# A recurrent cell on one Trainium2 core: biases as one row through TensorE, wx's first part in two column halves, and another deal of the inner weight sums

## The chip, the core and the metric

The kernel runs on one core of one Trainium2 chip. A core has five engines that run side by side and wait for one another through semaphores: TensorE (PE in the profile, with its weight loads as PEld) for matmuls, VectorE (DVE), ScalarE (ACT), GpSimd (POOL) and SyncE (SP), which here only issues transfers. Sixteen DMA engines move data between the device's memory and the on-chip memory. The metric is the device time of one execution in microseconds; the time before is the median of three runs.

## The reference

A recurrent cell goes over 512 steps for a batch of 8, with 512 inputs and 512 units, and its states are added to the input:

```python
def step(h, x_t):
    fused = sigmoid(concatenate([x_t, h], axis=-1) @ w_W + w_b)
    hidden_state, output_state = split(fused, 2, axis=-1)
    memory_state = x_t @ wx_W + wx_b + hidden_state * (h @ wh_W + wh_b)
    h_new = output_state * h + (1.0 - output_state) * tanh(memory_state)
    return h_new, h_new
...
out = x + scan(step, h0=cond_1024, over the 512 steps)
```

Everything is in 32-bit floats. There are three bias vectors: `w_b` (two gates), `wx_b` and `wh_b`.

## The kernel before

**Layout.** The 512 units are spread over 128 partitions as 4 groups (index `j`) of 32 partitions, so a matmul with a weight tile of 32 columns fills one quarter of the partitions, and four of them, one for each `j`, run beside one another. The contraction over 512 is cut into 4 chunks (index `k`). `wx` holds the weights that meet the input (384 columns for each `k` and `j`), `wa` and `wd` those that meet the state (256 and 128 columns). The banks of PSUM are named `xp0`, `xp1`, and `A`, `D`, `H` of two sets, `banks[0]` and `whole[1]`.

**The steps.** For every time step `i` TensorE multiplies the state by `wa` and `wd` (banks A, D and H, in the order of the string `ORDER`), and behind that does a few units of the input's part for later steps (x work): three units in most steps, four in the steps of `PLAIN` and in one of sixteen later. VectorE transposes what comes out (the transposes `tr`, `tz`, `md1`), ScalarE applies the sigmoids and the tanh, and two scans on VectorE give the new state `hT`, which TensorE's next step waits for. GpSimd adds the input to the state (`ot`), and SP stores it.

**The input's part.** For steps 0 to 31 it is made by plain passes: `x_pass(g, k)` multiplies four steps (group `g`) of the input by chunk `k` of `wx`. A bank is first filled with the bias by ScalarE (`seed`), and the passes add to it. From step 15 on the x work is done by a scheme with fewer products, for which sums of pieces of `wx` are wanted: `tw` (`weight_sum`, before step 0) and `ti` (`inner_weight`). VectorE makes the last 46 half pieces of `ti` at the ends of steps 0 to 15; the list `late` says which in which step.

**The start.** All engines begin together. SP issues the transfers in the order of the code, each up to 0.5 us of its time: `head` (the biases, already repeated over all partitions, then the first half chunk of the input and the first state), chunk 0 of `wx`, a piece of the input, chunks 1 to 3 of `wx`, `wa`, and `wd`; from the ninth on, the issue of one waits until the one eight places ahead has landed. TensorE meanwhile clears the banks: matmuls with the bfloat16 tile `none`, which is all zeros, and for bank D of `whole[1]` two matmuls with the float tile `zeros`. ScalarE waits for `head` and then seeds five banks from it. TensorE's first passes go through the chunks `k` in order, with the groups 0 to 3 inside (two groups in the last chunk), and then begins step 0, whose matmuls are dealt between passes that are still owed (the string `FIRST`); its D part needs `wd`. VectorE fills tiles, copies the first state out of `head` and makes the `tw` sums as the chunks of `wx` land. GpSimd copies parts of the bias from `head` into `xs` and `off`.

From the making of the banks on, the order on each engine is that of the code, and a wait holds back all that stands behind it on its engine.

Of the kernel before, what the change touches and what calls it, by code (L numbers as in the profile page):

```python
# [7 lines left out]
F32 = mybir.dt.float32  # L8
# [5 lines left out]
P = 128  # L14
NQ = 4
GS = 4
B = 8
# [15 lines left out]
HALF = 192  # L33
# [32 lines left out]

DONE = (5, 9, 14)

COLS = slice(64, 448)

SC = slice(128, 512)
# [5 lines left out]
def tile_cond_rnn_residual(  # L77
    ctx: ExitStack,
    tc: tile.TileContext,
    x: bass.AP,  # L80
    xh: bass.AP,
    wx_d: bass.AP,
    wa_d: bass.AP,
    wd_d: bass.AP,
# [31 lines left out]
    nc = tc.nc  # L116
# [4 lines left out]
    const = ctx.enter_context(tc.tile_pool(name="const", bufs=1))  # L121
# [6 lines left out]


    NX = NQ * TC * B // 2  # L130
    head = const.tile([P, 512 + NX + NQ * B], F32, name="head")
    nc.sync.dma_start(out=head, in_=xh)
    bias = head[:, :512]
    hin = head[:, 512 + NX :].rearrange("p (k b) -> p k b", k=NQ)

    def load_x(c, half=slice(0, 2), ks=slice(0, NQ)):

        if c < NCH:
            if c not in xins:
                xins[c] = xin_p.tile([P, 2, NQ, TC * B // 2], F32, tag="xin", name=f"xin_{c}")  # L140
            nc.sync.dma_start(
                out=xins[c][:, half, ks],
                in_=x[c].rearrange("p (e k n) -> p e k n", e=2, k=NQ)[:, half, ks],
            )

    def x_of(c, k, t, n):

        e, t = divmod(t, TC // 2)
        if c == 0 and e == 0:
            first = head[:, 512 : 512 + NX].rearrange("p (k n) -> p k n", k=NQ)  # L150
            return first[:, k, t * B : (t + n) * B]
        return xins[c][:, e, k, t * B : (t + n) * B]


    wx = const.tile([P, NQ, NQ, 384], F32, name="wx")
    for k in range(NQ):
        nc.sync.dma_start(out=wx[:, k], in_=wx_d[k])
        if k == 0:
            load_x(0, 1)

    wa = const.tile([P, NQ, NQ, 256], F32, name="wa")
    for k in range(NQ):
# [3 lines left out]
    wd = const.tile([P, NQ, NQ, 128], F32, name="wd")  # L166
# [16 lines left out]
    hd0 = [[pair(n, f"hd0{n}{i}", m, 3) for i in range(2)] for n, m in (("A", B), ("B", 32))]  # L183
    zeros = const.tile([P, 512], F32, name="zeros")
    nc.vector.memset(zeros, 0.0)  # L185
    none = const.tile([P, 128], BF16, name="none")
    nc.vector.memset(none, 0.0)

# [7 lines left out]
    idle = const.tile([P, IDLE], F32, name="idle")  # L196

    tw = const.tile([P, 4, 2, NQ, HALF], F32, name="tw")
    ti = const.tile([P, 7, 4, 2, HALF], F32, name="ti")
# [14 lines left out]
    whole = [{n: psum.tile([P, 512], F32, name=f"{n}{q}") for n in BANKS} for q in range(2)]  # L214
    banks = [{n: whole[q][n][:, :w] for n, w in BANKS.items()} for q in range(2)]
    xps = [psum.tile([P, 512], F32, name=f"xp{q}") for q in range(2)]

    def mm(out_, lhsT, rhs, start=False):
        nc.tensor.matmul(  # L219
            out_, lhsT, rhs, start=start, stop=False, skip_group_check=True  # L220
        )


    for t_ in xps + [whole[1]["H"], whole[1]["A"]] + list(banks[0].values()):
        mm(t_, none, none[:, :1].broadcast_to([P, t_.shape[1]]), start=True)
    for n in range(2):
        mm(whole[1]["D"], zeros[:, :128], zeros, start=n == 0)

    def bank_of(g):

# [60 lines left out]
    def seed(g):  # L291

        at = COLS if g else slice(0, 512)
        nc.scalar.copy(bank_of(g)[:, at], bias[:, at])

    def passes(*todo):

        for v in todo:
            x_pass(*v)
            yield  # L300
# [151 lines left out]
    def take(it, n=None):  # L452
        while n is None or n > 0:
            if next(it, it) is it:
                return
            n = None if n is None else n - 1
# [35 lines left out]
    jobs, late = {}, {}  # L492
# [2 lines left out]
        jobs.setdefault(i, []).extend(todo)  # L495

    halves = [(n, p, h) for n in (0, 2, 1, 3) for p in range(7) for h in range(2) if n or p > 4]
    for at in range(0, len(halves), 3):
        for n, p, h in halves[at : at + 3]:
            todo = late.setdefault(at // 3, [])  # L500
            if h and todo and todo[-1][:2] == (n, p):
                todo[-1] = (n, p, slice(0, 2))
            else:
                todo.append((n, p, slice(h, h + 1)))
    drains = {}
    for c in range(2, NCH):
        w0 = TC * c - LEAD
# [16 lines left out]
    for i in range(T):  # L524
        g, s = divmod(i, GS)
        c, t = divmod(i, TC)
        ps = banks[g % 2]
        if c > 0 and t in (1, 4, 7, 10):
            e, k = divmod(t // 3, 2)
# [5 lines left out]
        for n in (ORDER if i else FIRST).split():  # L535
# [6 lines left out]
            bank, k = n[0], int(n[1])  # L542
# [272 lines left out]
```

## Time and profile before

| | |
|---|---|
| median of the runs | 1627.92 us (1627.80 to 1628.28) |
| the profiled execution | 1627.71 us, of which its span is 1625.9 |
| mean granted TensorE clock | 1.000 |
| busy: TensorE, VectorE, ScalarE, GpSimd | 99%, 87%, 63%, 33% |
| first x pass on TensorE, from the start of the span | 6.30 us |
| first matmul of step 0 on TensorE | 16.23 us |
| one step later on | 3.12 us |

How to read it: rows of the timeline give the start, the length, the engine, the line of the kernel, the operation with its output and input, shapes and a count, and in brackets how long the engine had been idle before it and what ended that. A row of stretches gives the stretch, its length, TensorE's busy time with the count of its matmuls, the granted clock, the busy share of the DMA engines and GB/s. A row of a tile gives the count, the shortest, the median and the longest time in ns, and the first and the last start in us. One matmul of the code in 32-bit floats is two in the profile. In the DMA view a queue's row gives packets, MB, and the time that the packets took as a share of 16 engines over the stretch; the line of sizes counts packets cumulatively. A busy TensorE is not TensorE at its peak, since matmuls overlap and their ends are modelled.

### The profile page before, as it was taken

The page shows a single profiled execution, that of the slowest core. Times are in us where ns is not written, and L with a number is a line of the kernel's source. Part 1 is how long each engine was busy: PE and PEld are TensorE (multiplying, and loading weights), DVE is VectorE, ACT ScalarE, POOL GpSimd, SP SyncE. Part 2 cuts the span into 40 slices and gives each one's busy share as a digit, 9 for nine tenths or more (in the row PEclk, how much of TensorE's full clock was granted, in tenths as well). Part 3 has the DMA queues.
Part 4 walks back from the last instruction along what each step waited for, and adds up shares of the span by engine and source line. Part 5 has one row for each costly group of instructions (what it writes and reads, how often), then busy time and mean ns, then how long its engine had stood idle before and what let it go on. Part 6 is the DMA issues. An engine that isn't in the chain of part 4 may idle for free.

```text
span 1625.9 us, 120027 instructions
## 1 busy us (share of the span) xinstructions
PE 1616.3 (99%) x49211; PEld 1308.3 (80%) x49211; DVE 1411.1 (87%) x11757; ACT 1023.8 (63%) x6033; POOL 539.1 (33%) x1443
## 2 busy tenths in 40 slices
PE   9999999999999999999999999999999999999998
PEld 5888888888888888888888888888888888888876
DVE  8988888888888888888888888888888888888887
ACT  4666666666666666666666666666666666666665
POOL 2323333333333333333333333333333333333321
PEclk9999999999999999999999999999999999999999
DMA  4011111111111111111111111111111111110110
GB/s 192 12 40 33 29 37 38 43 32 33 31 43 39 35 34 31 39 38 39 33 29 37 38 43 32 30 35 43 38 33 34 32 39 38 39 34 25 31 35 10
DMA packets 66217, 62.04 MB, mean 38 GB/s; under 512 B 9856, under 2 KB 64000, under 8 KB 65664
## 3 DMA queue, kind: packets, MB, share of 16 engines
q1 hardware_dynamic: 65664, 54.35, 12.7%
q8 instruction: 385, 6.31, 1.7%
q14 instruction: 168, 1.38, 0.3%
HBM read 14.96 MB, written 8.39 MB: 14 GB/s over the span
## 4 chain that ended last, share of the span: by engine, by line
PE 98%; DVE 1%; issue 0%; ACT 0%; DVEq 0%
PE A L219 49%; PE D L219 27%; PE xp L219 16%; PE H L219 7%; DVE tr L577 0%; DVE m L565 0%; DVE md1B L636 0%; DVE hT L565 0%; DVE md1A L592 0%; DVE tz L577 0%; DVE zeros L185 0%; DVE hd0B L629 0%; DVE md1B L592 0%; DVE idle L600 0%; ACT hT L285 0%
## 5 line engine op out<-in xcount | busy, mean ns | idle before, releaser
L219 PE MATMUL A<-wa,hT 128*32 128x256 f32 x16352 | 877.8, 355 | 4.2 <-DVE hT L565 4.2
L219 PEld LDWEIGHTS A<-wa,hT 128*32 128x32 f32 x16352 | 497.5, 123 | 260.2 <-DVE hT L565 135.6
L219 PE MATMUL D<-wd,hT 128*32 128x128 f32 x16384 | 541.0, 273 | 0.0
L219 PEld LDWEIGHTS D<-wd,hT 128*32 128x32 f32 x16384 | 480.4, 122 | 21.8 <-DMA wd<-in_wd_dram 0.5
L731 POOL TENSOR_TENSOR ot<-xin,hT 128x32 f32<-128x32 f32 x503 | 134.4, 267 | 1046.5 <-DVE hT L565 1028.8
L285 ACT ACTIVATE md0A<-tr 128x16 f32<-128x16 f32 x512 | 112.9, 221 | 385.2 <-DVE tr L577 385.2
L285 ACT ACTIVATE hT<-m 128x8 f32<-128x8 f32 x2048 | 324.2, 207 | 46.8 <-DVE m L565 0.4
L577 DVE STREAM_TRANSPOSE tr<-A 128x64 f32<-128x64 f32 x511 | 127.8, 250 | 199.4 <-PE A L219 198.2
L285 ACT ACTIVATE hT<-hT 128x16 f32<-128x16 f32 x1024 | 232.3, 227 | 91.4 <-DVE hT L565 89.9
L219 PE MATMUL H<-wa,hT 128*32 128x64 f32 x8208 | 208.3, 219 | 0.0
L285 ACT ACTIVATE md0B<-tr 128x8 f32<-128x8 f32 x1024 | 160.0, 206 | 42.6 <-DVE tr L577 1.2
L219 PEld LDWEIGHTS H<-wa,hT 128*32 128x32 f32 x8208 | 185.6, 122 | 0.0
L565 DVE TENSOR_TENSOR_SCAN hT<-hd0B,hT 128x24 f32<-128x24 f32 x1024 | 171.4, 208 | 0.8 <-DVE hT L565 0.8
L565 DVE TENSOR_TENSOR_SCAN hT<-hd0A,hT 128x24 f32<-128x24 f32 x1024 | 171.9, 168 | 0.0
L565 DVE TENSOR_TENSOR_SCAN m<-md0B,md1B 128x24 f32<-128x24 f32 x1024 | 154.5, 193 | 0.5 <-issue 0.4
L629 DVE STREAM_TRANSPOSE hd0B<-sz 128x32 f32<-128x32 f32 x1024 | 148.5, 190 | 0.0
L565 DVE TENSOR_TENSOR_SCAN m<-md0A,md1A 128x16 f32<-128x16 f32 x1024 | 142.5, 181 | 5.1
L219 PE MATMUL xp<-ti,si 128*32 128x192 f32 (+1 forms) x3120 | 146.7, 295 | 0.0
L450 POOL TENSOR_TENSOR xs<-ff 128x192 f32<-128x192 f32 x240 | 139.5, 597 | 0.1
L636 DVE STREAM_TRANSPOSE md1B<-A 128x64 f32<-128x64 f32 x511 | 130.1, 255 | 0.0
L285 ACT ACTIVATE hd0A<-tz 128x16 f32<-128x16 f32 x512 | 116.6, 228 | 21.2
L592 DVE STREAM_TRANSPOSE md1B<-H 128x64 f32<-128x64 f32 x512 | 128.3, 251 | 0.0
(110 smaller groups left out, 1861.0 us busy)
## 6 DMA issues: line engine op xcount, KB each, us to landing
ff<-tt SPq DMA_DIRECT2D x120, 96.0 KB, 2.6
ff<-tt SPq DMA_DIRECT2D x120, 72.0 KB, 2.2
out_dram<-ot SPq DMA_DIRECT2D x128, 64.0 KB, 1.8
xin<-in_x_dram SPq DMA_DIRECT2D x112, 64.0 KB, 2.1
ff<-ff SPq DMA_DIRECT2D x60, 96.0 KB, 2.1
ff<-ff SPq DMA_DIRECT2D x60, 72.0 KB, 2.7
wx<-in_wx_dram SPq DMA_DIRECT2D x4, 768.0 KB, 7.3
wa<-in_wa_dram SPq DMA_DIRECT2D x4, 512.0 KB, 11.1
```

Source lines behind the costliest of these rows:

```text
L219: nc.tensor.matmul(out_, lhsT, rhs, start=start, stop=False, skip_group_check=True)
L285: inst = nc.scalar.activation(out_, in_, func, **kw).ins
L450: nc.gpsimd.tensor_tensor(to, a, b, ALU.add)
L565: return nc.vector.tensor_tensor_scan(*[t_[:, :, c_].rearrange("p n c s -> p (n c s)") for t_ in (out_, d0, d1)], 0.0, ALU.mult, ALU.add,).ins
L577: inst = nc.vector.transpose(t_.rearrange("p c n -> p (c n)"), raw[n][hf]).ins
L592: inst = nc.vector.transpose(md1[hf][g % 2][:, :, :, hf].rearrange("p n c -> p c n"), raw["h"][hf]).ins
L629: nc.vector.transpose(hd0[1][i % 2][:, :, q, 2], sz[:, 32 * q : 32 * q + 32]).ins
L636: nc.vector.transpose(md1[1][g % 2][:, :, :, 0].rearrange("p n c -> p c n"), ps["A"][:, :HU])
L731: pool_done[i + 1] = nc.gpsimd.tensor_tensor(ot[:, t], x_of(c, slice(0, NQ), t, 1), hTs[(i + 1) % NH][:, :, :, B * s1 : B * s1 + B, 2].rea ...
```

## The change

It has three parts, all at the start.

First, `head` no longer carries the biases. They come as one row of 2048 floats on one partition, by a transfer of their own that stands first on SP's queue. The row is put into the memory of `ti`, which is not otherwise written before the inner sums. Four matmuls with a column of ones (`ones`, one partition by 32) repeat it over the partitions of the first bank `xp0`, and ScalarE copies that bank into a new tile `bias`, from which everything reads that read `head` before. Bank `xp0` then already holds its bias, so its seed goes; the other seeds stay. Bank D of `whole[1]` is cleared by a `none` matmul like the other banks, and the two `zeros` matmuls go.

Second, chunk 0 of `wx` is loaded in two halves of 192 columns of each `j`, the piece of the input between them, and its passes are done in the same halves: all four groups with the first half, then all four with the second.

Third, the list `SUMS` says how many half pieces of `ti` each of the first sixteen steps makes; before it was three in each and one in the last. The pieces keep their order.

```diff
+SUMS = (3, 3, 3, 2, 2, 4, 2, 4, 4, 4, 3, 2, 3, 2, 4, 1)
...
-    head = const.tile([P, 512 + NX + NQ * B], F32, name="head")
+    ti = const.tile([P, 7, 4, 2, HALF], F32, name="ti")
+    rows_b = ti[:1].rearrange("p a n j c -> p (a n j c)")[:, : NQ * 512]
+    nc.sync.dma_start(out=rows_b, in_=bias_d)
+    head = const.tile([P, NX + NQ * B], F32, name="head")
     nc.sync.dma_start(out=head, in_=xh)
-    bias = head[:, :512]
-    hin = head[:, 512 + NX :].rearrange("p (k b) -> p k b", k=NQ)
+    bias = const.tile([P, 512], F32, name="bias")
+    hin = head[:, NX:].rearrange("p (k b) -> p k b", k=NQ)
...
     wx = const.tile([P, NQ, NQ, 384], F32, name="wx")
-    for k in range(NQ):
-        nc.sync.dma_start(out=wx[:, k], in_=wx_d[k])
-        if k == 0:
+    for v in range(2):
+        nc.sync.dma_start(out=wx[:, 0, :, HALF * v : HALF * v + HALF], in_=wx0_d[v])
+        if v == 0:
             load_x(0, 1)
+    for k in range(1, NQ):
+        nc.sync.dma_start(out=wx[:, k], in_=wx_d[k - 1])
...
+    ones = const.tile([1, 32], F32, name="ones")
+    nc.vector.memset(ones, 1.0)
...
-    for t_ in xps + [whole[1]["H"], whole[1]["A"]] + list(banks[0].values()):
+    for t_ in xps + list(whole[1].values()) + list(banks[0].values()):
         mm(t_, none, none[:, :1].broadcast_to([P, t_.shape[1]]), start=True)
-    for n in range(2):
-        mm(whole[1]["D"], zeros[:, :128], zeros, start=n == 0)
+    for j in range(NQ):
+        mm(xps[0][32 * j : 32 * j + 32], ones, rows_b[:, 512 * j : 512 * j + 512])
+    nc.scalar.copy(bias, xps[0])
...
-    for g in range(5):
+    for g in range(1, 5):
         seed(g)
-    take(passes(*[(g, k) for k in range(NQ) for g in range(2 if k == NQ - 1 else 4)], (4, 0)))
+    take(passes(*[(g, 0, slice(v, v + HALF)) for v in (0, HALF) for g in range(4)]))
+    take(passes(*[(g, k) for k in range(1, NQ) for g in range(2 if k == NQ - 1 else 4)], (4, 0)))
...
-    for at in range(0, len(halves), 3):
-        for n, p, h in halves[at : at + 3]:
-            todo = late.setdefault(at // 3, [])
+    for at, n_ in enumerate(SUMS):
+        todo = late.setdefault(at, [])
+        for n, p, h in halves[:n_]:
...
+        del halves[:n_]
...
-    xh_d = c_(_np.concatenate([_np.repeat(bias_d, 32, 0), xd[0, :, : 2 * TC * Bn], h0], 1))
+    xh_d = c_(_np.concatenate([xd[0, :, : 2 * TC * Bn], h0], 1))
+    bias_d = c_(bias_d.reshape(1, -1))
+    wx0_d = c_(_np.stack([wx_d[0, :, :, :192], wx_d[0, :, :, 192:]]))
+    wx_d = c_(wx_d[1:])
```

What this makes of the order on the engines, at the places that matter below. SP's queue at the start, before (`xin_74` and `xin_81` are the input's first two chunks):

```order
L132 DMA head<-in_xh_dram 128x800
L157 DMA wx<-in_wx_dram 128x1536
L141 DMA xin_74<-in_x_dram 128x256
L157 DMA wx<-in_wx_dram 128x1536 x3
L163 DMA wa<-in_wa_dram 128x1024
L141 DMA xin_81<-in_x_dram 128x256
L163 DMA wa<-in_wa_dram 128x1024 x3
L167 DMA wd<-in_wd_dram 128x1536
```

and SP's queue now:

```order
L137 DMA ti<-in_bias_dram 1x2048
L139 DMA head<-in_xh_dram 128x288
L164 DMA wx<-in_wx_dram 128x4x192
L148 DMA xin_77<-in_x_dram 128x256
L164 DMA wx<-in_wx_dram 128x4x192
L168 DMA wx<-in_wx_dram 128x1536 x3
L172 DMA wa<-in_wa_dram 128x1024
L148 DMA xin_85<-in_x_dram 128x256
L172 DMA wa<-in_wa_dram 128x1024 x3
L176 DMA wd<-in_wd_dram 128x1536
```

The bias row stands first, `head` is shorter, and chunk 0 of `wx` is two transfers of 4 runs of 192 floats on each partition; what follows keeps its order.

TensorE behind the first matmuls with `none`, before (`xp_175` and `xp_176` are the banks xp0 and xp1, `H_174` and `A_172` the banks of groups 2 and 3):

```order
L219 MATMUL H_171<-none 128x64
L219 MATMUL D_173<-zeros 128x512 x2
L219 MATMUL xp_175<-wx,head 32x384 x4
L219 MATMUL xp_176<-wx,head 32x384 x4
L219 MATMUL H_174<-wx,xin_74 32x384 x4
L219 MATMUL A_172<-wx,xin_74 32x384 x4
L219 MATMUL xp_175<-wx,head 32x384 x4
```

and TensorE at the same place now (`xp_180`, `xp_181`, `H_179` and `A_177` are the same four banks):

```order
L229 MATMUL H_176<-none 128x64
L229 MATMUL xp_180<-ti,ones 32x512 x4
L229 MATMUL xp_180<-wx,head 32x192 x4
L229 MATMUL xp_181<-wx,head 32x192 x4
L229 MATMUL H_179<-wx,xin_77 32x192 x4
L229 MATMUL A_177<-wx,xin_77 32x192 x4
L229 MATMUL xp_180<-wx,head 32x192 x4
L229 MATMUL xp_181<-wx,head 32x192 x4
L229 MATMUL H_179<-wx,xin_77 32x192 x4
L229 MATMUL A_177<-wx,xin_77 32x192 x4
L229 MATMUL xp_180<-wx,head 32x384 x4
```

The `zeros` matmuls are gone, the four with `ones` stand in their place, and chunk 0 has twice the passes at half the columns.

On ScalarE the first copy at the start now reads bank xp0, which TensorE writes, where it read `head`, and the four seeds behind it read its output.

VectorE at the end of step 4, before (the first row is the last scan of the state, `ti` the inner sums, `tr_5` the first transpose of step 5):

```order
L565 TENSOR_SCALAR hT_95<-hd0B_108,hT_94 128x24 x2
L338 TENSOR_TENSOR ti<-tw 128x384
L338 TENSOR_TENSOR ti<-tw 128x192
L710 MEMSET idle 128x1 x2
L577 STREAM_TRANSPOSE tr_5_850<-A_172 128x64
```

and at the same place now:

```order
L579 TENSOR_SCALAR hT_99<-hd0B_112,hT_98 128x24 x2
L349 TENSOR_TENSOR ti<-tw 128x192 x2
L724 MEMSET idle 128x1 x2
L591 STREAM_TRANSPOSE tr_5_874<-A_177 128x64
L606 STREAM_TRANSPOSE md1A_107<-A_177 128x64
```

Step 4 ends with two half pieces where it had three (a whole piece of 384 columns counts two).

More of the change, by code (lines that the diff above doesn't have):

```diff
@@ L80, in tile_cond_rnn_residual @@
     x: bass.AP,
+    bias_d: bass.AP,
     xh: bass.AP,
+    wx0_d: bass.AP,
     wx_d: bass.AP,
@@ L149, in x_of @@
         if c == 0 and e == 0:
-            first = head[:, 512 : 512 + NX].rearrange("p (k n) -> p k n", k=NQ)
+            first = head[:, :NX].rearrange("p (k n) -> p k n", k=NQ)
             return first[:, k, t * B : (t + n) * B]
@@ L198, in tile_cond_rnn_residual @@
     tw = const.tile([P, 4, 2, NQ, HALF], F32, name="tw")
-    ti = const.tile([P, 7, 4, 2, HALF], F32, name="ti")
     so = [const.tile([P, 4, 2, 2, 32], F32, name=f"so{q}") for q in range(2)]
@@ L504, in tile_cond_rnn_residual @@
                 todo.append((n, p, slice(h, h + 1)))
+        del halves[:n_]
+    assert not halves
     drains = {}
@@ L801 @@
     for name, a in (
-        ("x", xd), ("xh", xh_d), ("wx", wx_d), ("wa", wa_d), ("wd", wd_d), ("wd3", wd3_d),
+        ("x", xd), ("bias", bias_d), ("xh", xh_d), ("wx0", wx0_d), ("wx", wx_d), ("wa", wa_d), ("wd", wd_d), ("wd3", wd3_d),
     ):
```

## The prediction

> **What bounds the kernel now.** I read the page's busy shares and its chain first, then the chain in order of time for the first 50 us, then the steps, then the start in the timeline, and last the DMA view, since the change touches nothing but the start and the sums in the first sixteen steps.
>
> ```profile
> PE 1616.3 (99%) x49211; PEld 1308.3 (80%) x49211; DVE 1411.1 (87%) x11757; ACT 1023.8 (63%) x6033; POOL 539.1 (33%) x1443
> ...
> PE 98%; DVE 1%; issue 0%; ACT 0%; DVEq 0%
> ```
>
> TensorE carries 98% of the chain. To see whether single steps hide something, I cut the trace at the starts of successive `tr<-A` transposes (one per step) and asked for TensorE's busy time between them.
>
> ```profile
> 27.71:30.87 3.16, 3.16 (x116) 1.00 0.03 8
> 30.87:33.97 3.10, 3.10 (x113) 1.00 0.02 5
> 33.97:37.16 3.19, 3.19 (x116) 1.00 0.08 21
> 37.16:40.43 3.27, 3.27 (x124) 1.00 0.03 8
> 40.43:43.91 3.48, 3.48 (x131) 1.00 0.02 5
> 43.91:47.02 3.11, 3.11 (x116) 1.00 0.02 5
> ...
> 78.67:81.79 3.12, 3.12 (x108) 1.00 0.02 5
> ```
>
> A step with three units of x work takes 3.10 to 3.12 us and one with four units (steps 5 to 9 and 14) 3.27: a period set by TensorE's own work. Only the first rows deviate: step 2 by 0.05, step 4 by 0.08, and steps 6 and 7 together by 0.05 (3.48 + 3.11 against 2 x 3.27). About 500 steps are left alone by the change, so all that can move is the start, here in the timeline (start us, length us, engine, line).
>
> ```profile
> 0.74 0.39 SPq L132 DMA_DIRECT2D head<-in_xh_dram  x1
> ...
> 1.93 0.15 PEld L219 LDWEIGHTS <-none 128*128 128x128 bf16 x1 [0.28 <-issue]
> ...
> 2.36 0.15 PEld L219 LDWEIGHTS <-none 128*128 128x128 bf16 x1 [0.28 <-issue]
> ...
> 3.60 2.77 PE L219 MATMUL D<-zeros 128*128 128x512 f32 x4
> ...
> 4.93 0.48 ACT L294 COPY H<-head 128x384 f32<-128x384 f32 x1
> ...
> 5.35 0.47 ACT L294 COPY A<-head 128x384 f32<-128x384 f32 x1
> ...
> 6.30 0.16 PEld L219 LDWEIGHTS xp<-wx,head 128*32 128x32 f32 x8 [0.76 <-ACT A L294]
> ...
> 8.72 0.33 SPq L167 DMA_DIRECT2D wd<-in_wd_dram  x1
> ...
> 8.91 1.47 PE L219 MATMUL xp<-wx,head 128*32 128x384 f32 x16
> ...
> 17.59 0.19 PEld L219 LDWEIGHTS xp<-wa,hT 128*32 128x32 f32 x8 [0.51 <-DMA wa<-in_wa_dram]
> ...
> 20.68 0.84 PEld L219 LDWEIGHTS D<-wd,hT 128*32 128x32 f32 x32 [0.53 <-DMA wd<-in_wd_dram]
> ```
>
> The x passes begin at 6.30, as the `zeros` matmuls leave TensorE (3.60 + 2.77 = 6.37), chunk k=1 of wx is used from 8.91, and step 0 stands still for `wd` at 20.68. The chain gives the price of TensorE's work between:
>
> ```profile
> 7.80 0.65 PE H L219 x8
> 8.45 0.65 PE A L219 x8
> ...
> 19.43 0.33 PE xp L219 x8
> 19.76 0.45 PE H L219 x32
> ```
>
> One x pass of 384 columns is 0.645 us, one k of step 0's A 0.33, its H 0.45. From 6.30 to 20.68 lie 19 passes (12.26), four A (1.32) and H: 14.03 of 14.38 us. So TensorE has only 0.35 us of idle time there, the waits for `wa` and `wd`, and transfers and TensorE arrive almost together. A gain on one alone is stopped by the other; a loss on TensorE is free up to 0.35.
>
> ```profile
> DMA packets 2034, 7.15 MB, mean 397 GB/s; under 512 B 219, under 2 KB 589, under 8 KB 2033
> ...
> q1 hardware_dynamic: 2033, 7.14, 100.1%
> ```
>
> That is the stretch from 2 to 20 us: the 16 DMA engines are never free, so the time at which `wd` lands is the sum of what is queued ahead of it.
>
> ```profile
> wd<-in_wd_dram SPq DMA_DIRECT2D x1, 768.0 KB, 11.9
> ```
>
> Issued at 8.72, landed 11.9 later: 20.62, the 20.68 above.
>
> **The transfers.** Three edits. Bytes: 512 bias columns leave `head`, 128 x 2048 B = 262 KB, and one row of 8 KB comes in: 254 KB less at 397 GB/s, -0.64 us. Issue: the row's DMA stands ahead of `head` on SP's queue, and everything moves behind it by one issue, +0.39 (the `head` row). The lower end is 0, if the later issues catch up; the upper is +0.71, if the 8 KB run on one DMA engine (0.32 at the rate worked out next). Rows: chunk 0 of wx was 128 runs of 6144 B and becomes 2 x 512 runs of 768 B. No such run is in the trace, but these three stretches (8 to 10, 12 to 14 and 134.2 to 137.5 us) bound it:
>
> ```profile
> q1 hardware_dynamic: 153, 0.84, 101.1%
> ```
> ```profile
> DMA packets 324, 0.80 MB, mean 399 GB/s; under 512 B 33, under 2 KB 161, under 8 KB 324
> ...
> q1 hardware_dynamic: 324, 0.80, 102.1%
> ```
> ```profile
> q1 hardware_dynamic: 432, 0.20, 20.7%
> ```
>
> First: 1.011 x 16 x 2 us for 0.84 MB is 38.5 ns per KB, so 236 ns for a 6144 B run. Second: 128 runs of 1 KB (161 less 33 short ones) and 0.67 MB of long ones; 32.7 less 25.8 us leaves 54 ns per 1 KB run. Third: two xin loads and a store, 384 runs of 512 B in 10.9 us, 28.5 ns each. Between the two neighbours 768 B takes 41 ns; ends 29.6 (the long runs' rate) and 54. Over 16 engines, 1024 x 41 is 2.62 us against 1.89 (128 x 236) before: +0.73, ends 0 and +1.57. The sum, with the middle of each: -0.64 + 0.39 + 0.73 = +0.48 us; ends -0.64 and +1.64. The second half's DMA is one more issue (0.4 us), but SP issues `wd` 12 us ahead, so that costs nothing.
>
> The Trainium skill, "DMA: Bandwidth & Descriptors", section "Why small descriptors are slow (HBM only)", puts about 3 cycles on each packet beside one per 32 bytes, which would make a 768 B run 27 cycles for 24 and the split about +0.2 us (an estimate), the transfers -0.05 in all. The 512 B rows disagree: 28.5 ns against 19.7 at the long runs' rate is 44% more, where that rule has 19%.
>
> **TensorE and ScalarE at the start.** Removed: two `zeros` matmuls (2.77 us). Added: one more `none` matmul of 512 columns, 0.43 (2.36 - 1.93), and a small memset ahead on VectorE, about 0.06, so the work that began at 3.60 begins at 4.09. The bias matmuls that now stand there, and all passes behind them, wait for the bias row, whose DMA takes `head`'s place at 0.74; `head` itself landed 3.2 us after its issue, at 3.9, and 8 KB should not take longer:
>
> ```profile
> head<-in_xh_dram SPq DMA_DIRECT2D x1, 400.0 KB, 3.2
> ```
>
> Four matmuls of 512 columns follow. Their speed is unsure, because equal instructions took unequal times here:
>
> ```profile
> L219 PE MATMUL D<-zeros x4: 592/757/1202, 3.6 to 5.8; 128*128 128x512 f32 x4
> ...
> L219 PE MATMUL xp<-wx,head x64: 486/486/510, 6.3 to 15.1; 128*32 128x384 f32 x64
> ```
>
> The slowest of the `zeros` took twice the fastest; from 6.3 on all passes are alike. By an x pass the four bias matmuls are 0.645 x 512/384 = 0.86 us, at half speed 1.72; I take 1.29, as they lie where the `zeros` changed speed. A matmul lasts 486 ns where four of them pass in 0.32 us, so 0.16 is added until the last one is out, and they end at 5.54 (5.11 to 5.97). ScalarE then copies the bank into `bias`:
>
> ```profile
> L294 ACT COPY xp<-head x4: 477/483/590, 4.0 to 22.5; 128x384 f32<-128x384 f32 x3, 128x512 f32<-128x512 f32 x1
> ```
>
> 0.59, to 6.13, and the first pass may not touch that bank before. Its three further seeds read `bias`, so they queue behind: done at 6.61, 7.03, 7.45 (0.48, then 0.42 apart as 4.93 and 5.35 are). Half passes are 0.32 each: 6.2 to 6.5, 6.65, 7.1, and 7.5 to 7.8, then four of the second half without a wait, 9.11. That is 0.20 later than 8.91 (ends -0.23 and +0.63): starting earlier is eaten by the seeds. The 0.35 us of idle time takes it up, so the price at `wd` is 0.
>
> GpSimd's copies from `bias`, which waited for `head` before, begin about 2.2 us later, at 6.1, and stay hidden, as do ScalarE's seeds, in these idle times (the brackets):
>
> ```profile
> 15.02 0.20 ACT L314 COPY H<-xp 128x64 f32<-128x64 f32 x1 [8.12 <-PE xp L219]
> ...
> 23.87 0.52 POOL L731 TENSOR_TENSOR ot<-head,hT 128x32 f32<-128x32 f32 x1 [15.86 <-DVE hT L565]
> ```
>
> VectorE's first `tw` sum now waits for both halves of chunk 0, but it waits for chunk 1 behind that anyway.
>
> **The inner sums.** The same 46 halves: steps 3, 4, 6, 11 and 13 lose one, 5, 7, 8, 9 and 14 gain one.
>
> ```profile
> 42.90 1.08 DVE L338 TENSOR_TENSOR ti<-wx,ti 128x384 f32<-128x384 f32 x2
> ...
> L338 DVE TENSOR_TENSOR ti<-wx,ti x8: 321/537/626, 42.9 to 62.0; 128x384 f32<-128x384 f32 x4, 128x192 f32<-128x192 f32 x4
> ```
>
> A half is about 0.32 us of VectorE. What can be won is the lateness of the steps that lose one: 0.08 (step 4) and 0.05 (6 and 7), -0.13 us. The steps that gain one have 0.16 us more TensorE work under which part of it hides, and step 6 shows that 0.21 of lateness in such a pair is mostly given back. Ends -0.25 (all the lateness of the first rows) and +0.2 (two steps pushed by 0.1).
>
> **Sum.** `wd` +0.48, TensorE 0 beside it, sums -0.13: +0.35 us. The profiled execution took 1627.71 us (a span of 1625.9 and 1.8 around it), 0.2 under the median 1627.92; it becomes 1628.06, and the median 1628.3.
>
> **Rivals.**
> Covered: 768 B runs cost little more than long ones, the transfers come out even, and TensorE's lateness fits into its idle time. Only the sums are left, -0.13: 1627.8. For it: a continuous stream; against it: the 28.5 ns rows.
> Faster: no price for the short runs and the extra issue caught up, so `wd` is 0.64 earlier, and full speed for the bias matmuls, so chunk 1 starts at 8.68. TensorE would be ready for `wd` at 20.68 - 0.35 - 0.23 = 20.10: -0.58, with the sums -0.25, about 1627.2. It needs both; one alone gives nothing.
> Slower, by TensorE's speed: without the `zeros` TensorE idles between 5.5 and 7.5, and stays in the half speed of the first `zeros` record. If it does so through the first half passes, these take 0.64 instead of 0.32, the start of chunk 1 slips by 1.3 more, 1.5 in all, 1.15 past the idle time; with the sums +1.0: 1628.9 (at most 2.4 us, if all eight half passes are slow). It decides once chunk 1 begins after 9.74 (8.91 + 0.35 + 0.48). Against it: the granted clock reads 1.00 in every row above. The Trainium skill, "TensorE: Matmul & The Clock Gate", section "Part 1: The HAM clock gate (the "warmup" mystery)", says that the array starts at half rate and is released after about 3.4 us of activity; the `zeros` times agree, the clock column doesn't.
> A shift in every step: another place of the tiles in memory costs or saves something 511 times. It takes 6.4 ns a step to pass 0.2%; TensorE's period of 3.12 speaks against it.
>
> **Chances.** Forecast 0.44 (1627.9 to 1628.9 with the run price's ends), covered 0.20, faster 0.18, TensorE's speed 0.13, every step 0.05. 0.2% is 3.3 us, about what a measurement of this kernel can tell from no change; the first four stay within it. So faster 0.02, same 0.94, slower 0.04. The range reaches from the faster case, 1627.2, to 1629.6, where the transfers' upper end (1.64 - 0.13) lies and most of the half speed.
>
> **What would show it.** Right: `wd` used at about 21.2; 28.5 to 54 ns per 768 B run, in a busy stream; chunk 1 begun near 9.1 to 9.4 after seeds that end at 7.5; steps 4, 6 and 7 at 3.11 and 3.27; every later step 3.12. Wrong: `wd` at 20.7 or before, x passes that last longer than 0.33 for half the columns, or a changed period after step 16.

## The result, and the profile after

The changed kernel takes 1631.38 us (median; 1630.62 to 1632.01), the kernel before beside it 1628.16 us (1627.74 to 1628.46). The ratio is 1.0019, with a 95% interval of 1.0012 to 1.0027: 2.0 to 4.4 us slower. That is above the predicted range, 1627.2 to 1629.6. The profiled execution took 1630.62 us, with a span of 1628.8 against 1625.9. In two of the experiments below one execution of eleven was far slower (7775.70 us in `none_d`, 2101.39 us in `w_runs`); their ratios leave it out, their medians hold it.

TensorE's busy share and its part of the chain read almost as before, from the page of the changed kernel:

```profile
PE 1618.3 (99%) x49248; PEld 1309.9 (80%) x49248; DVE 1412.0 (87%) x11762; ACT 1024.3 (63%) x6033; POOL 540.8 (33%) x1443
...
PE 97%; DVE 2%; issue 0%; ACT 0%; POOL 0%; DVEq 0%
```

VectorE has one per cent more of the chain; the page says no more than that. The starts of the steps say where the time went. Step 1, by its first transpose, starts at 26.26 us where it started at 24.59: +1.67. The lateness stays at 1.68 up to step 5, grows to 2.40 by step 16 (+0.72), and wanders between 2.2 and 2.7 from there on (2.62 at the last step), with steps of 3.12 us in both. So the loss has two main places, the start and the steps with dealt sums. A third, small one is the end: from the first transpose of the last step to the end of the span it is 4.89 us before and 5.18 now (+0.29). In all kernels below that issue as many transfers as the kernel before it is 4.88 to 4.90, with one transfer more 5.05 or 5.06, and in `bw`, with two more, 5.17.

The start of the changed kernel in the timeline:

```profile
4.19 1.93 PE L229 MATMUL xp<-ti,ones 1*32 1x512 f32 x8
...
6.18 0.59 ACT L238 COPY bias<-xp 128x512 f32<-128x512 f32 x1 [3.96 <-PE xp L229]
...
6.82 1.51 PE L229 MATMUL xp<-wx,head 128*32 128x192 f32 x16 [0.70 <-ACT bias L238]
...
8.10 0.87 PE L229 MATMUL H<-wx,xin 128*32 128x192 f32 x8
...
9.38 1.16 PE L229 MATMUL xp<-wx,head 128*32 128x192 f32 x16
10.08 0.33 SPq L176 DMA_DIRECT2D wd<-in_wd_dram  x1
...
10.37 0.50 PE L229 MATMUL H<-wx,xin 128*32 128x192 f32 x8
...
10.70 0.50 PE L229 MATMUL A<-wx,xin 128*32 128x192 f32 x8
...
11.02 1.46 PE L229 MATMUL xp<-wx,head 128*32 128x384 f32 x16
...
22.34 0.17 PEld L229 LDWEIGHTS D<-wd,hT 128*32 128x32 f32 x4 [0.16 <-issue]
```

The four `ones` matmuls (each stands as two records) take 1.93 us. Two half passes lie between 6.82 and 8.10, one each between 8.10, 8.74 and 9.38: 0.64 us for 192 columns. At 10.37 and 10.70 the same form takes 0.33. Nothing waits in between; TensorE works at half its speed until about 10.05 us. Chunk 1 of `wx`, used from 8.91 before, is used from 11.02. `wd` is not waited for any more: its row at 22.34 names issue, not a DMA. It was issued at 10.08 and took 11.8, from the DMA view of the first 24 us:

```profile
wd<-in_wd_dram SPq DMA_DIRECT2D x1, 768.0 KB, 11.8
```

That is 21.88, which is 1.26 behind the 20.62 of before. The clock column shows nothing of the half speed. In the view by stretches (start and end, length and TensorE's busy time, granted clock, DMA share, GB/s), 6.82 to 9.38 holds four half passes, 10.04 to 11.02 three:

```profile
6.82:9.38 2.56, 2.56 (x32) 1.00 1.03 399
9.38:10.04 0.66, 0.66 (x15) 1.00 0.95 391
10.04:11.02 0.98, 0.98 (x28) 1.00 1.04 433
```

The same view for the steps 5 to 9:

```profile
38.84:42.18 3.34, 3.34 (x124) 1.00 0.03 7
42.18:45.44 3.26, 3.26 (x120) 1.00 0.00 0
45.44:48.95 3.51, 3.51 (x129) 1.00 0.02 5
48.95:52.32 3.37, 3.37 (x120) 1.00 0.09 26
52.32:55.90 3.58, 3.58 (x128) 1.00 0.02 5
```

Steps 5, 7, 8 and 9, which now hold four halves of the inner sums, take 3.34 to 3.58 in place of 3.27 (3.11 in step 7, which followed a long step 6). TensorE counts as busy throughout, though it can't have more work; what it waits for stands on VectorE, here at the end of step 9 (scan of the state, inner sums, first transpose of step 10):

```profile
54.21 0.34 DVE L579 TENSOR_TENSOR_SCAN hT<-hd0B,hT 128x24 f32<-128x24 f32 x2
...
54.58 1.38 DVE L349 TENSOR_TENSOR ti<-tw,ti 128x192 f32<-128x192 f32 x3
...
55.90 0.24 DVE L591 STREAM_TRANSPOSE tr<-A 128x64 f32<-128x64 f32 x1
```

The step began at 52.32, and the sums start 2.26 us later. In the kernel before, where this step began at 50.29, they start 2.27 us later, and three halves stand there:

```profile
52.56 0.86 DVE L338 TENSOR_TENSOR ti<-tw,ti 128x192 f32<-128x192 f32 x2
```

Three halves end at 3.13 of 3.27; four end at 3.64, and the next step's transpose stands behind them.

### The profile page after: what moved, and what is told of

Its sections match the earlier page's. It is cut to its first block, busy times and chain, and to the rows that moved or that the text cites. A ratio compares the mean times of both kernels' runs of the same rounds, so it can differ in the third digit from the quotient of the medians.

```text
span 1628.8 us, 120107 instructions
## 1 busy us (share of the span) xinstructions
PE 1618.3 (99%) x49248; PEld 1309.9 (80%) x49248; DVE 1412.0 (87%) x11762; ACT 1024.3 (63%) x6033; POOL 540.8 (33%) x1443
## 4 chain that ended last, share of the span: by engine, by line
PE 97%; DVE 2%; issue 0%; ACT 0%; POOL 0%; DVEq 0%
PE A L229 48%; PE D L229 26%; PE xp L229 16%; PE H L229 7%; DVE tr L591 0%; DVE m L579 0%; DVE ti L349 0%; DVE md1B L650 0%; DVE hT L579 0%; DVE md1A L606 0%; DVE tz L591 0%; DVE hd0B L643 0%; ACT md0B L296 0%; POOL si L383 0%; ACT bias L238 0%
```

## The experiments

Each is timed against the kernel before on the same chip. The ratio's interval is about plus or minus 0.0009, which is 1.5 us, so a median alone separates little. The verdicts rest on the traces, with the medians as support. "Late at step 1" is the start of step 1, in the one trace of each kernel, against the trace of the kernel before.

### Parts of the change alone: sums, bias row, halves, and both loads

`s_only`: only the table of counts.

```diff
+SUMS = (3, 3, 3, 2, 2, 4, 2, 4, 4, 4, 3, 2, 3, 2, 4, 1)
...
-    for at in range(0, len(halves), 3):
-        for n, p, h in halves[at : at + 3]:
...
+    for at, n_ in enumerate(SUMS):
...
+        for n, p, h in halves[:n_]:
...
+        del halves[:n_]
```

> The kernel before with the new deal of the inner sums alone. Theory (a fourth half piece does not fit into a step of 3.27 us): about +0.7 us, with steps 5, 7, 8, 9 and 14 lengthened as in the changed kernel and the start unmoved (step 1's first transpose at 24.6). Rival (the prediction's term): -0.1 us.

Median 1628.16 against 1627.86: ratio 1.0002 (0.9993 to 1.0011). In the trace the lateness grows by 0.65 us between steps 5 and 16, at the same steps as in the changed kernel:

```profile
37.86:41.19 3.33, 3.33 (x124) 1.00 0.03 7
...
44.45:47.94 3.49, 3.49 (x128) 1.00 0.03 6
47.94:51.29 3.35, 3.35 (x120) 1.00 0.10 26
51.29:54.89 3.60, 3.60 (x128) 1.00 0.02 5
```

So the new counts cost by themselves in these steps. In the whole time it can't be made out: the median's +0.30 has 1.5 us on either side. The start, which this kernel does not touch, is 0.70 late as well: its `zeros` matmuls took 3.59 us in place of 2.77. The moment at which TensorE gets fast differs from execution to execution.

`b_only`: the bias row and the `ones` matmuls, with `wx` whole and the old counts.

```diff
-    head = const.tile([P, 512 + NX + NQ * B], F32, name="head")
...
+    nc.sync.dma_start(out=rows_b, in_=bias_d)
+    head = const.tile([P, NX + NQ * B], F32, name="head")
...
-    for n in range(2):
-        mm(whole[1]["D"], zeros[:, :128], zeros, start=n == 0)
+    for j in range(NQ):
+        mm(xps[0][32 * j : 32 * j + 32], ones, rows_b[:, 512 * j : 512 * j + 512])
+    nc.scalar.copy(bias, xps[0])
...
```

> The bias row, the ones matmuls and the none matmul in place of the zeros ones alone; wx in whole chunks, the old deal of the sums. Theory (TensorE runs at half speed until about 10 us, since the zeros work is gone): first passes of 384 columns take 1.29 us instead of 0.645, chunk 1 begins near 11, the time rises by 1.7 to 2.4 us. Rival (the late transfers of the 768 B runs are what costs): nothing of that here, 0 +- 0.3 us, passes of 0.645.

Median 1629.18 against 1627.86: 1.0010 (1.0001 to 1.0019). The passes in the timeline:

```profile
4.18 1.93 PE L226 MATMUL xp<-ti,ones 1*32 1x512 f32 x8
...
6.82 2.79 PE L226 MATMUL xp<-wx,head 128*32 128x384 f32 x16 [0.70 <-ACT bias L235]
...
8.16 0.33 SPq L173 DMA_DIRECT2D wd<-in_wd_dram  x1
...
9.38 1.51 PE L226 MATMUL H<-wx,xin 128*32 128x384 f32 x8
...
10.66 1.46 PE L226 MATMUL A<-wx,xin 128*32 128x384 f32 x8
...
11.94 1.48 PE L226 MATMUL xp<-wx,head 128*32 128x384 f32 x16
```

A pass of 384 columns takes 1.28 (half of 9.38 - 6.82) up to the last one of chunk 0, and 0.645 afterwards. Chunk 1 begins at 11.94, step 1 is 2.60 late. `wd`, issued at 8.16 and 12.2 under way, landed at 20.36, 0.26 earlier. The two other kernels with these transfers, `b_zeros` and `b_fill` below, land it at 20.41 and 20.43, and those with the transfers of before between 20.39 and 20.62: a gain in the direction that the bytes say, of 0.13 in the mean, with ranges that touch. TensorE was not there to use it.

`w_only`: chunk 0 of `wx` in two halves of its columns, 512 runs of 768 B each, and nothing else.

```diff
-        nc.sync.dma_start(out=wx[:, k], in_=wx_d[k])
-        if k == 0:
+    for v in range(2):
+        nc.sync.dma_start(out=wx[:, 0, :, HALF * v : HALF * v + HALF], in_=wx0_d[v])
+        if v == 0:
...
+    for k in range(1, NQ):
+        nc.sync.dma_start(out=wx[:, k], in_=wx_d[k - 1])
...
```

> Chunk 0 of wx in two halves and its passes in halves alone; biases in head, zeros matmuls kept, old sums. Theory of TensorE's speed: half passes of 0.32 us from the first on, and only the transfers cost: chunk 1 lands 0.7 to 1.4 later, +0.4 to +1.0 us in time. Rival (transfers are the whole cause): +1.7 us. Second rival (a pass of half the columns is itself slow): 0.64 for each half pass here too, +2 us.

Median 1628.32 against 1627.86: 1.0004 (0.9995 to 1.0012). Here TensorE waits for the loads, twice:

```profile
10.22 1.50 PE L222 MATMUL xp<-wx,head 128*32 128x384 f32 x16 [0.27 <-DMA wx<-in_wx_dram]
...
22.63 0.84 PEld L222 LDWEIGHTS D<-wd,hT 128*32 128x32 f32 x32 [0.55 <-DMA wd<-in_wd_dram]
```

Chunk 1 lands at 10.2 (8.7 before), `wd` is used at 22.63 (20.68): +1.95. Its half passes take 0.32 us from the first on, and step 1 is 1.66 late by the loads alone. The price of a run, from the stretch from 4 to 5 us:

```profile
DMA packets 362, 0.28 MB, mean 283 GB/s; under 512 B 19, under 2 KB 362, under 8 KB 362
...
q1 hardware_dynamic: 362, 0.28, 98.2%
```

16 engines times 0.982 us over 343 packets (the 19 short ones left out) is 46 ns, against the forecast's 41. But this stretch is above the rest. All 1024 runs of 768 B of this trace take 42.4 ns in the mean, and 984 of them exactly 36; 27 take more than 54, the longest 912. With 29.6 at the long runs' rate the mean makes 1024 x 12.8 / 16 = 0.82 us for the two halves (0.41 if all took 36), where the forecast had 0.73. About 1.1 of the 1.95 at `wd` isn't explained by it.

`bw`: the changed kernel with the old counts.

```diff
-SUMS = (3, 3, 3, 2, 2, 4, 2, 4, 4, 4, 3, 2, 3, 2, 4, 1)
+SUMS = (3, 3, 3, 3, 3, 3, 3, 3, 3, 3, 3, 3, 3, 3, 3, 1)
```

> The changed kernel with the old deal of the sums. Theory: the parts add up, +3.2 - 0.7 = +2.5 us, steps after the first as in the kernel before. Rival (the sums cost nothing, the start all): +3.2 us.

Median 1630.05 against 1627.86: 1.0015 (1.0006 to 1.0024). Step 1 is 2.18 late and the lateness is the same at step 16: without the new counts nothing is lost in those steps. Its half passes take 0.64 us until about 11.0, though the start is the changed kernel's to the letter, where they did until 10.05. The loads differ as much:

```profile
23.15 0.84 PEld L229 LDWEIGHTS D<-wd,hT 128*32 128x32 f32 x32 [0.47 <-DMA wd<-in_wd_dram]
```

`wd`, issued at 11.13 in place of 10.08, is waited for until 23.15, 2.5 later than in the kernel before, where the changed kernel with the same transfers has +1.26. So one trace does not fix the price of these transfers to better than about 1 us.

The medians above the kernel before are +0.30 (sums), +0.46 (halves), +1.32 (bias row), +2.19 (both loads) and +3.22 (all). The three parts make 2.08 of the 3.22; with 1.5 us on either side of each, that neither shows nor refutes that they add up. At the start they don't: step 1 is 2.60 late with the bias row alone, 1.66 with the halves alone, and 2.18 and 1.67 in the two kernels with both. Nor does all of a late start reach the end of a trace: between step 16 and the last step the lateness of the kernels here changes by -0.9 to +0.2 us (`w_only` goes from 1.65 to 0.71), as single steps in different places take 0.1 to 0.3 us longer.

### Is it TensorE's speed?

Theory: TensorE starts at half speed, and the `zeros` matmuls kept it at work until it got fast; `ones` and the gap behind them don't. The rival: what delays is the work put in (bias matmuls, ScalarE's copy), and the pass times are a matter of the data's arrival.

`none_d`: the kernel before with one `none` matmul in place of the two with `zeros`. It does 2.3 us less on TensorE (2.77 - 0.43) and changes no transfer.

```diff
-    for t_ in xps + [whole[1]["H"], whole[1]["A"]] + list(banks[0].values()):
+    for t_ in xps + list(whole[1].values()) + list(banks[0].values()):
...
-    for n in range(2):
-        mm(whole[1]["D"], zeros[:, :128], zeros, start=n == 0)
```

> The kernel before with one none matmul in place of the two zeros matmuls, all else as before: TensorE has 2.4 us less work ahead of its first pass. Theory (TensorE speeds up only after some microseconds of dense work, and the zeros matmuls are that work): passes can start near 6.0 but run at 1.29 us each for several microseconds, chunk 1 begins at 10 to 11.5 instead of 8.9, the time rises by 0.8 to 2 us. Rival (speed does not depend on the work ahead): passes of 0.645 from 6.0 on, 0 to -0.3 us.

Median 1630.04 against 1628.04: 1.0010 (1.0001 to 1.0019). By the ratio it is 1.6 us slower (0.2 to 3.1) with less to do, and step 1 is 2.60 late:

```profile
6.54 2.79 PE L219 MATMUL xp<-wx,head 128*32 128x384 f32 x16 [2.32 <-DMA wx<-in_wx_dram]
...
9.07 1.53 PE L219 MATMUL H<-wx,xin 128*32 128x384 f32 x8
...
10.35 1.47 PE L219 MATMUL A<-wx,xin 128*32 128x384 f32 x8
...
11.63 1.48 PE L219 MATMUL xp<-wx,head 128*32 128x384 f32 x16
```

All four passes of chunk 0 take 1.28 us, with nothing waited for behind the first. The theory holds: the useless matmuls bought speed.

`b_zeros`: `b_only` with the `zeros` pair put back ahead of `ones`.

```diff
+    for n in range(2):
+        mm(whole[1]["D"], zeros[:, :128], zeros, start=n == 0)
     for j in range(NQ):
         mm(xps[0][32 * j : 32 * j + 32], ones, rows_b[:, 512 * j : 512 * j + 512])
```

> The bias row alone (as in b_only) with the two zeros matmuls put back between the none and the ones matmuls, which adds 2.4 to 3.2 us of TensorE work ahead of the first pass. Theory of TensorE's speed: ones and passes run at full speed (ones in 1.0, passes 0.645), the first pass starts near 8.2 to 8.7 and chunk 1 near 10.8 to 11.3, about as early as or earlier than in b_only (11.94): 0 to -0.8 us against b_only, in spite of more work. Rival (the late start of the passes is what costs, at whatever speed): +1.5 to +2.4 us over b_only.

Median 1629.21 against 1628.04: 1.0008 (0.9999 to 1.0017).

```profile
3.64 3.48 PE L226 MATMUL D<-zeros 128*128 128x512 f32 x4
...
7.06 1.06 PE L226 MATMUL xp<-ti,ones 1*32 1x512 f32 x8
...
8.82 1.50 PE L226 MATMUL xp<-wx,head 128*32 128x384 f32 x16 [0.71 <-ACT bias L237]
```

`ones` takes 1.06 in place of 1.93, the passes run at full speed from the first (two in 1.32), and chunk 1 begins at 11.43, before the 11.94 of `b_only`, although 2.9 us more work stands ahead of `ones`. Most of what the speed gives back, the later start of the passes (8.82) takes: step 1 is 2.07 late where `b_only` has 2.60. The medians (+1.17 here, +1.32 there) can't tell that apart.

`b_fill`: `b_only` with two `none` matmuls between `ones` and the passes, so that TensorE doesn't stand still there.

```diff
+    for n in range(2):
+        mm(whole[1]["D"], none, none[:, :1].broadcast_to([P, 512]), start=True)
     nc.scalar.copy(bias, xps[0])
```

> b_only with two more none matmuls behind the ones matmuls, in the 0.7 us in which TensorE waits for ScalarE's copy. If the idle gap is what keeps TensorE slow: speed-up by 8.5 us, chunk 1 near 9.7, about -1.5 us against b_only. If the ones matmuls themselves (one row, 32 columns) do not count as dense work: speed-up still between 9.5 and 11.6, -0.5 to +0.2 us against b_only.

Median 1629.67 against 1628.04: 1.0011 (1.0002 to 1.0020). TensorE gets fast near 11.6 us, where it does at 11.9 in `b_only`, and not by 8.5. The gap isn't the reason. It had worked from 1.57 us without a pause, 10 us. In the kernels with `zeros` the change came within those four records: they took 2.48 us at the least (one slow record of 0.86, three of 0.43 and 0.3 until the last is out: changed at about 4.6) and 3.72 at the most (all slow, until 7.2), which is 3.1 to 5.7 us behind the first matmul at 1.53. Counted from the end of `ones` it took 5.6 in `b_fill`. So the matmuls with one row and 32 columns didn't bring the speed nearer. The other kernels without `zeros` agree: from their first x pass, behind `ones` or a gap, the change took 3.2 us in the changed kernel, 4.2 in `bw` and 5.1 in `b_only` and `none_d`, about the 3.1 to 5.7 that the kernels with `zeros` need from their first matmul.

### Why are the halves' transfers late?

`w_runs`: `w_only` with tile and memory laid out so that each half is 128 runs of 3072 B.

```diff
-    wx = const.tile([P, NQ, NQ, 384], F32, name="wx")
+    wx = const.tile([P, NQ, 2, NQ, HALF], F32, name="wx")
...
-        nc.sync.dma_start(out=wx[:, 0, :, HALF * v : HALF * v + HALF], in_=wx0_d[v])
+        nc.sync.dma_start(out=wx[:, 0, v], in_=wx0_d[v])
```

> w_only with wx laid out so that each half of chunk 0 is one run of 3072 B on a partition (as many transfers, the same half passes, 256 runs instead of 1024). Theory (the price of the halves is that of the short runs): chunk 1 lands near 8.8 instead of 10.2, wd is used at 20.7 to 21 instead of 22.6, the time is that of the kernel before within 0.4 us. Rival (the second transfer itself, or the half passes, cost): as w_only, wd near 22.5.

Median 1628.29 against 1628.04: 1.0002. In this trace the long runs did not cure it: `wd` is issued at 10.44 and used at 22.83, as late as with the short ones.

```profile
10.47 1.50 PE L222 MATMUL xp<-wx,head 128*32 128x384 f32 x16 [0.34 <-DMA wx<-in_wx_dram]
...
22.83 0.84 PEld L222 LDWEIGHTS D<-wd,hT 128*32 128x32 f32 x32 [0.51 <-DMA wd<-in_wd_dram]
```

`w_one`: short runs, but one transfer; passes over whole columns.

```diff
-        nc.sync.dma_start(out=wx[:, k], in_=wx_d[k])
...
+    nc.sync.dma_start(
+        out=wx[:, 0].rearrange("p j (v c) -> p j v c", v=2), in_=wx0_d.rearrange("v p j c -> p j v c")
+    )
...
```

> The kernel before, with chunk 0 of wx still in one transfer and passes over whole columns, but read in 1024 runs of 768 B (the two halves of its columns lie apart in memory). Theory run length: short runs delay everything queued behind, so chunk 1 lands near 10.2 us as with two transfers of such runs, wd is issued near 10.2 and step 0 waits for it to about 22.6; the time is near +0.4 us. Rival, two transfers: the second transfer of chunk 0, behind the input piece, is what delays; in one transfer only the price of the runs is left, at most +0.7 us at 46 ns a run: chunk 1 by 9.4, wd near 21.3, and the time within +0.2 us of before.

Median 1628.89 against 1627.76: 1.0008 (0.9999 to 1.0017). `wd` is issued at 9.89 and used at 22.19:

```profile
9.89 0.33 SPq L170 DMA_DIRECT2D wd<-in_wd_dram  x1
...
22.19 0.85 PEld L222 LDWEIGHTS D<-wd,hT 128*32 128x32 f32 x32 [0.55 <-DMA wd<-in_wd_dram]
```

In this trace short runs in one transfer are enough for +1.2 at chunk 1 and +1.5 at `wd`, more than the runs' own price: they take 38.1 ns in the mean here, which makes 0.54 us.

`w_pair`: `w_runs` with the two halves one behind the other and the input piece of 1 KB runs behind both.

```diff
-        if v == 0:
-            load_x(0, 1)
+    load_x(0, 1)
```

> The kernel before, with chunk 0 of wx in two transfers of 128 x 4 columns blocks of 3072 B runs, as in the run with long halves, but the second half issued directly behind the first and the input piece behind both. Theory interleaving: the 1 KB runs of the input piece between the halves made the rate sag to 200 GB/s at 4.0 to 4.9 us, and without them chunk 1 lands by 9.0 and wd by 21. Rival, two transfers: splitting alone costs, chunk 1 lands at 10.2 to 10.5 and wd near 22.7 whatever the order. Time in the first case within 0.15 us of before, in the second +0.2 to +0.4.

Median 1627.68 against 1627.76: 0.9999 (0.9990 to 1.0008). `wd` is issued at 9.59 and used at 21.33:

```profile
21.33 1.05 PEld L221 LDWEIGHTS D<-wd,hT 128*32 128x32 f32 x32 [0.26 <-DMA wd<-in_wd_dram]
```

That lies between the two expectations: +0.65 at `wd` where `w_runs` has +2.15. These traces point to both the runs' length and the order of two transfers around the 1 KB runs of the input, and in the changed kernel both are there. They don't show it: one trace of each stands here, and the same transfers gave values 1.05 us apart in the changed kernel and `bw`. Part of the delay is that the 16 DMA engines stand idle: from 1 us to the landing of `wd` 0.6 us in the kernel before, 0.8 in `w_pair`, 0.9 in `w_one`, 1.3 in `w_only` and 2.0 in `w_runs`. Why they do so where the runs are long isn't settled. Kernels with the transfers of before vary too. Their `wd` was issued between 8.26 and 8.89 us, and that of the three kernels with the bias row and `wx` whole between 8.16 and 9.03.

### Can four halves be avoided, and can TensorE be fast earlier?

`s_star`: counts without a four.

```diff
+SUMS = (3, 3, 3, 3, 2, 3, 2, 3, 3, 3, 3, 3, 3, 3, 3, 3)
```

> The kernel before with the halves of the inner sums dealt 3 to every step but 2 at steps 4 and 6, and 3 at step 15: no step holds four. Theory VectorE's period: about 2.16 us of a step's own work, 0.1 to 0.46 of transposes and 0.25 to 0.33 a half let three halves into 3.27 us and not four, so nothing is lost at steps 5 to 15 and steps 4 and 6 shed 0.05 to 0.1: lateness of step 16 against the kernel before, less that of step 1, is -0.1 us, where the new deal has +0.65 to +0.74. Rival: any changed order costs, whatever the counts: +0.3 or more. Time: -0.1 us, against +0.3 with the new deal.

Median 1628.10 against 1627.76: 1.0003 (0.9994 to 1.0012). Steps 5 to 10, then 15:

```profile
37.11:40.38 3.27, 3.27 (x124) 1.00 0.03 8
...
50.19:53.46 3.27, 3.27 (x124) 1.00 0.03 8
53.46:56.98 3.52, 3.52 (x124) 1.00 0.01 2
...
69.59:72.88 3.29, 3.29 (x112) 1.00 0.03 7
```

The five steps of 3.27 are undisturbed, as the theory has it. But the sum of it is +0.5 by step 16, not -0.1. Step 15, which got three halves in place of one beside its transposes, loses 0.18 (3.29 for 3.11), which the theory should have told. Step 10, with three halves as before, loses 0.36: its second scan of the state comes 0.28 us late behind the first, which the kernel before doesn't have there. What causes it stays open; the kernel with the same counts below has it at the same step, so "any changed order costs", the rival, isn't ruled out. Of the relief, step 4 shows none (3.19 as before), and steps 6 and 7 together give 0.05.

`star_early`: the same counts, and `none` cleared ahead of `zeros`, so that the first matmuls start earlier.

```diff
-    zeros = const.tile([P, 512], F32, name="zeros")
-    nc.vector.memset(zeros, 0.0)
     none = const.tile([P, 128], BF16, name="none")
     nc.vector.memset(none, 0.0)
+    zeros = const.tile([P, 512], F32, name="zeros")
+    nc.vector.memset(zeros, 0.0)
```

> The kernel before with that same deal of the inner sums, and the zeroing of `none` ahead of that of `zeros` on VectorE, so that TensorE's first matmuls start about 0.4 us earlier. Theory TensorE's speed: its fast state comes 3.3 to 5 us after steady work begins, so it comes earlier, the passes begin at 5.9 in place of 6.3 and less of them is slow in those executions in which the change of speed is late; step 0 still waits for wd at 20.6. The time is 0.2 to 0.6 us under before. Rival: wd alone sets step 1, and only the sums' -0.1 is left.

Median 1627.79 against 1627.76: 1.0003 (0.9994 to 1.0012), no gain. The `zeros` matmuls begin at 3.06, not 3.60, but take 3.38 us, and the passes begin at 6.36: an earlier start of the same slow work left the passes where they were. No version here beats the kernel before.

## Why the prediction was wrong

**TensorE 0 beside it: wrong, the largest miss.** The sum had `ones` at 1.29 us, "as they lie where the `zeros` changed speed", and the half passes at 0.32. Both were slow: `ones` 1.93, and five of the eight half passes 0.64. The passes began at 6.82 for 6.2 (+0.62), the five cost 5 x 0.32 = 1.60 more, and of the 0.35 us of waits for the seeds that the forecast had between the passes nothing is left: 9.11 + 0.62 + 1.60 - 0.35 = 10.98, measured 11.02. Past the 0.35 us of idle time that leaves 11.02 - 8.91 - 0.35 = 1.76, and step 1 is 1.67 late.

The rival "slower, by TensorE's speed" named this mechanism and its deciding point, chunk 1 after 9.74. It had a chance of 0.13 and a price of +1.0 with four slow passes. Its price was short by the later start of the passes (0.62, most of it the slow `ones`) and by the fifth pass (0.32). What spoke against it was the clock column's 1.00, and that was the error of judgement: the column reads 1.00 beside 0.64 and 0.33 for the same instruction. The records of unequal length, 592 to 1202 ns for `zeros`, were the evidence, and the work with nothing in it was to be read as having a use. The Trainium skill, "TensorE: Matmul & The Clock Gate", section "Part 1: The HAM clock gate (the "warmup" mystery)", has the array at half rate until one busy window of some 3.4 us has passed, and lets the windows run freely, so that the moment differs between executions. The traces agree with the half rate, 1.28 against 0.645 a pass, and with a moment that differs, 3.1 to 5.7 us from the first matmul with `zeros` behind it.

**The transfers +0.48 at `wd`: too low, inside their ends in the changed kernel's trace, outside them in `bw`'s.** `wd` landed 1.26 later, and 2.5 later in `bw`; the upper end was 1.64. Two terms were mis-sized. The halves' +0.73: the 1024 runs took 44.6 ns in the mean for the forecast's 41, which makes 0.96, though 941 of them took only 36; the rest lies in a few long ones. And the issue, +0.39, with the second half's put at nothing ("one more issue") because `wd` is issued 12 us ahead: that holds for engines that are "never free". In the changed kernel they were free early on, as the stretch from 1 to 10 us shows, before and now (columns as above):

```profile
1.00:10.00 9.00, 8.47 (x59) 1.00 0.90 345
```
```profile
1.00:10.00 9.00, 7.72 (x56) 1.00 0.79 261
```

That is 0.99 us more in which the DMA engines stood idle, all of it before 4 us, where their share is 0.74 before, 0.61 in `b_only` and 0.37 now. -0.64 + 0.99 + 0.96 = 1.31, for the measured 1.26. The likely reason, not tested by itself: the shorter `head` gives the engines less to do while SP needs 0.68 and 0.57 us to issue a half of 512 runs (0.42 a chunk of 128 runs before); with the long `head`, in `w_only`, the share before 4 us is 0.71.

In the changed kernel `wd` is there 0.46 before TensorE comes to it (21.88 against 22.34), so this loss is covered by the other. It was luck which of the two came last: `w_only`, with TensorE fast, has step 1 as late (1.66) by the loads, and `bw` waits for `wd` again.

**The inner sums -0.13: wrong in sign.** +0.72 in the changed kernel, +0.65 alone. The step that failed is that the steps that gain one "have 0.16 us more TensorE work under which part of it hides": the forecast compared a half's 0.32 with TensorE's longer step, but did not add up VectorE's own work in it. That sum was to be had from the trace of before: 2.27 us to the first piece and 0.86 for three halves leave 0.14 in a step of 3.27, and a half needs 0.23 to 0.55. The relief at the steps that lose one was real but small: step 6 fell from 3.48 to 3.26, but step 4 stayed at 3.20, and `s_star` shows that 6 and 7 together gain 0.05, as forecast.

**The steady state and the rest: right but for the end.** The later steps take 3.12; the seeds, GpSimd's copies and ScalarE's copy of the bias stayed where they were put, hidden or at 0.59. That "all that can move is the start" left out the end of the kernel, +0.29 with two transfers more.

**The sum.** 1.67 at the start, 0.72 in the sums and 0.29 at the end are 2.68 of the 2.9 by which the spans differ; the rest is spread over 500 steps, within what these change between the kernels here. The median's +3.22 lies at the bound of 3.3 that the chances used, with an interval on both sides of it. "Same" at 0.94 rested on each of the first four cases staying within about 1 us by itself; several misses of one sign passed that together. Two of the forecast's own figures don't follow from its terms, and nothing hangs on them: the faster case is 1627.92 - 0.58 - 0.25 = 1627.1, not 1627.2, and the run price's ends, 29.6 and 54 ns, span about 1627.5 to 1629.1, not 1627.9 to 1628.9.

## What to carry to other kernels

Ask of every useless instruction ahead of TensorE's first real work what it does to the speed of the work behind it, and read that speed from the durations of equal instructions, not from the clock column. An engine that is off the chain has a period of its own: before it is given a piece, add up its work in that step against the step's length, and not only the piece against the room of the bound engine. Where transfers and TensorE arrive together, take the larger of the two losses, and cost both at their unfavourable end.

## What had not been expected of the hardware

TensorE's change of speed is not fixed: the same four records of `zeros` end after 2.48 us in `s_star` and 3.72 in `w_pair`, and the changed kernel's start got fast at 10.05 in one kernel and at about 11.0 in the other. In the three kernels whose start is the same to the letter, the one before, `s_only` and `s_star`, step 1 begins 0.77 us apart (24.52 to 25.29). Matmuls with one row and 32 columns kept TensorE busy for 1.93 us and brought the change no nearer. Of the 1024 runs of 768 B, 925 to 988 take the same 36 ns; what makes their mean 38 to 52 from trace to trace is 18 to 60 that take more than 54, up to 1.5 us. And two transfers with long runs, placed around one with 1 KB runs, delayed `wd` in their one trace as much as short runs did.
